# A cross-attention block on one core: the calls of the way in put in another order

## The chip, the cores and the metric

The kernel runs on one core of a Trainium2 chip. The metric is the device time of one execution in microseconds (us). Five engines work side by side, each with its own queue of instructions: TensorE (PE; its weight loads are listed apart as PEld), VectorE (DVE), ScalarE (ACT), GpSimd (POOL) and SyncE (SP), which here does nothing but issue transfers. An engine executes its queue in order; between engines, semaphores make an instruction wait for what it needs.

## The reference, cut to what matters

```python
def _ada_ln(x, c, W_ss, b_ss):
    h = (x - mean(x)) / sqrt(var(x) + EPS)
    scale, bias = split(silu(c) @ W_ss + b_ss, 2)
    return (1.0 + scale)[:, None, :] * h + bias[:, None, :]

xq = _ada_ln(x_q, t_vec, Wss_q, bss_q)
xkv = _ada_ln(x_kv, t_vec, Wss_kv, bss_kv)
q = (xq @ Wq + bq).reshape(B, Lq, nh, dh)
kv = (xkv @ Wkv + bkv).reshape(B, Lkv, 2, nh, dh)
k, v = kv[:, :, 0], kv[:, :, 1]
scores = einsum('bqhd,bkhd->bhqk', q, k) / sqrt(dh)
out = einsum('bhqk,bkhd->bqhd', softmax(scores), v).reshape(B, Lq, H)
return x_q + (out @ Wp + bp)
```

Here B = 16, Lq = 1024, Lkv = 64, H = 512, nh = 16 and dh = 32, all in fp32. `t_vec` is one conditioning vector for each batch.

## The kernel before

**Tiling.** The queries are cut into 32 blocks (`NB`) of 512 rows, two for each batch. A block is held as four tiles of 128 rows, t = 0 to 3. The context is taken in two groups, "A" (batches 0 to 7) and "B" (8 to 15), of 8 × 64 = 512 rows each. They go through the same helpers as a block: load (`load_x`), statistics (`q_stats`), scale (`first_scale`, `q_scale`), normalisation (`hidden`), transposition (`turned_features` on PE for A and B, `turned_products` for block 0, `turn` on DVE with the transfers of `move` for the other blocks), and the scale and shift from the conditioning vector (`modulated`, `turned_scaled`, `scale_features`).

**Products.** Each projection, of q, k, v and of the output, is a 512 × 512 × 512 product done with seven products of half size instead of eight (`seven`, L526, matmul at L544; `product`, L932, matmul at L950), 8 matmuls each. The seven are taken in an order written out by hand, and their operands are partly sums and differences of halves: `column_sums` forms those of the weights on POOL, `feature_sums` those of the features (on DVE for A, on POOL for the others), `weight_sums` and `row_sums` those of the output projection on POOL. Their results are copied out or added up by `context_out`, `query_out`, `query_added` and `added`.

**Attention.** `score_products(i, z)` (matmul at L663) makes the scores of one half z of the keys of block i, with 32 × 32 tiles. `maximum` (DVE) and `copied` (ACT) read them; `maxima`, `subtract` (POOL), `weights` (ACT, the exponential), `total` (POOL), `row_total` and `inverse_rows` (DVE and four small transfers), `mix` (PE, L831) and `divided` (DVE) make the rest. In the notes below "score half" is one `score_products`.

**Tiles that are shared.** Four of them matter here.

- PSUM pool `ps_s` has two slots, each a pair of banks `[P, 2, TB]`. In `turned_features` the transposed tiles t = 0 and t = 2 are the two halves of one such tile, t = 1 and t = 3 of the other; `modulated(i, k, n, eng)` reads t = 2n when `eng` is VectorE and t = 2n + 1 when it is ScalarE. Semaphores follow the whole tile: a write to one half waits for the reads of the other half that stand ahead of it in the order, and a read of one half waits for a write of the other that stands ahead of it.
- The `x` slots are two, so `load_x(1)` waits until `turned_products` has read `x_0`, and `load_x(2)` until `turned_features("B", ·)` has read `x_B`.
- The slot `WT` holds `stage_A`, then `stage_B` (V on its way to `value_move`, 16 transfers for each group), then the weight sums `WT` of the output projection.
- `sum_0` (written by `total(0)`, read by `row_total(0)`) and the copied scores `s_1_0` share the slot `big2`.

```python
if t < 2:
    spares[i, t] = ps_s.tile([P, 2, TB], F32, tag="s", name=f"pxk_{i}_{t}")
turned[i, t] = spares[i, t % 2][:, t // 2, :]
...
t = 2 * n if eng is nc.vector else 2 * n + 1
...
src = turned[i, t][:, at : at + LKV]
```

**The order.** No planner runs in the kernel: each engine's queue holds its instructions in the order in which the Python calls stand. The calls of L987 to L1407, the way in, bring the groups A and B and the blocks 0 to 2 to the point where the loop over `i in range(3, NB - 2)` (L1409) can start. The loop interleaves the scores of block i with the output projection of block i − 2, the mix of i − 1 and the queries of i + 1. So at the end of the way in, block 0 is in its output projection, block 1 in its mix, block 2 in its softmax and block 3 has its queries.

Of the kernel before, what the change touches and what calls it, by code (L numbers as in the profile page):

```python
# [20 lines left out]
def cross_attention_block(  # L21
# [18 lines left out]
    nc = tc.nc  # L40
# [946 lines left out]
    column_sums("k", w_k_sb, w_k_sums, (2,))  # L987
    q_stats("A", (0,))
    q_stats("A", (1,))
    scale_shift_rows("kv", 0)  # L990
    first_scale(0)
    hidden("A", (0,))
    biases()
    scale_shift_taken("kv", 0)
    scale_shift("kv", 2 * NC, 0)
    turned_features("A", 0)
    hidden("A", (1,))
    column_sums("k", w_k_sb, w_k_sums, (0,))
    turned_features("A", 1)
    column_sums("k", w_k_sb, w_k_sums, (1,))  # L1000
    modulated("A", 0, 0, nc.scalar)
    modulated("A", 0, 0, nc.vector)
    q_stats("A", (3,))
    load_x("B")
    q_stats("A", (2,))
    first_scale(1)
    hidden("A", (2,))
    hidden("A", (3,))
    context_product("A", "k", 1)
    scale_shift_rows("kv", 1)  # L1010
    scale_shift_taken("kv", 1)
    turned_features("A", 2)
    context_out("A", "k", 1)
    column_sums("v", w_v_sb, wv_sums, (0,))
    scale_shift("kv", 2 * NC, 1)
    column_sums("v", w_v_sb, wv_sums, (2,))
    modulated("A", 1, 0, nc.vector)
    turned_features("A", 3)
    modulated("A", 1, 1, nc.vector)
    modulated("A", 1, 0, nc.scalar)  # L1020
    modulated("A", 0, 1, nc.scalar)
    modulated("A", 1, 1, nc.scalar)
    context_product("A", "k", 2)
    context_product("A", "v", 1)
    modulated("A", 0, 1, nc.vector)
    context_product("A", "v", 2)
    context_out("A", "k", 2)
    context_out("A", "v", 1)
    feature_sums("A", nc.vector, (0,))
    feature_sums("A", nc.vector, (1,))  # L1030
    feature_sums("A", nc.vector, (2,))
    column_sums("v", w_v_sb, wv_sums, (1,))
    load_query_weights()
    q_stats(0, (0,))
    context_out("A", "v", 2)
    context_product("A", "k", 7)
    context_out("A", "k", 7)
    scale_shift_rows("q", 0)
    context_product("A", "v", 6)
    q_stats(0, (2,))  # L1040
    q_stats(0, (3,))
    q_stats(0, (1,))
    q_scale(0)
    context_product("A", "v", 7)
    feature_sums("A", nc.vector, (3,))
    scale_shift_rows("q", 1)
    context_product("A", "k", 6)
    load_x(1)
    scale_shift_taken("q", 0, 2)
    hidden(0, (2,))  # L1050
    hidden(0, (3,))
    column_sums("v", w_v_sb, wv_sums, (3,))
    context_out("A", "v", 6)
    q_stats("B", (0,))
    q_stats("B", (2,))
    hidden(0, (1,))
    scale_shift("q", 0, 0, 2)
    context_product("A", "v", 5)
    hidden(0, (0,))
    column_sums("k", w_k_sb, w_k_sums, (3,))  # L1060
    q_stats("B", (1,))
    context_out("A", "v", 7)
    q_stats("B", (3,))
    column_sums("q", w_q_sb, w_q_sums, (0,))
    context_out("A", "v", 5)
    turned_products()
    context_out("A", "k", 6)
    context_product("A", "k", 5)
    context_product("A", "v", 3)
    turned_scaled(2)  # L1070
    context_out("A", "k", 5)
    q_scale("B")
    turned_scaled(3)
    column_sums("q", w_q_sb, w_q_sums, (2,))
    turned_scaled(1)
    turned_scaled(0)
    hidden("B", (0,))
    load_x(2)
    q_stats(1, (0,))
    hidden("B", (3,))  # L1080
    hidden("B", (1,))
    feature_sums(0, nc.gpsimd, (0,))
    q_stats(1, (2,))
# [5 lines left out]
    value_move("A", 0)  # L1089
    column_sums("q", w_q_sb, w_q_sums, (1,))  # L1090
    q_stats(1, (1,))
    context_out("A", "k", 3)
    hidden("B", (2,))
# [5 lines left out]
    feature_sums(0, nc.gpsimd, (1,))  # L1099
    modulated("B", 0, 0, nc.scalar)  # L1100
    context_product("A", "k", 4)
    context_out("A", "k", 4)
    modulated("B", 1, 1, nc.scalar)
    query_product(0, 1)
    context_product("B", "k", 1)
    modulated("B", 0, 1, nc.vector)
    context_out("A", "v", 4)
    modulated("B", 1, 1, nc.vector)
    modulated("B", 0, 1, nc.scalar)
    modulated("B", 1, 0, nc.vector)  # L1110
    feature_sums(0, nc.gpsimd, (2,))
    q_scale(1)
    load_projection_bias()
    query_seed(0)
    modulated("B", 1, 0, nc.scalar)
    hidden(1, (0,))
    query_product(0, 6)
    query_product(0, 2)
    context_out("B", "k", 1)
    hidden(1, (1,))  # L1120
    turn(1, (0,))
    column_sums("q", w_q_sb, w_q_sums, (3,))
    feature_sums("B", nc.gpsimd, (0,))
    turn(1, (1,))
    hidden(1, (2,))
    turn(1, (2,))
    hidden(1, (3,))
    feature_sums(0, nc.gpsimd, (3,))
    turn(1, (3,))
    query_out(0, 2)  # L1130
    context_product("B", "k", 2)
    context_out("B", "k", 2)
    q_stats(2, (0,))
    query_product(0, 7)
    q_stats(2, (1,))
    move(1, two=True)
    query_out(0, 6)
    q_stats(2, (2,))
    context_product("B", "k", 7)
    query_out(0, 7)  # L1140
    feature_sums("B", nc.gpsimd, (1,))
    q_stats(2, (3,))
    context_out("B", "k", 7)
    q_scale(2)
    hidden(2, (0,))
    feature_sums("B", nc.gpsimd, (2,))
    query_product(0, 5)
    feature_sums("B", nc.gpsimd, (3,))
    hidden(2, (1,))
    query_product(0, 4)  # L1150
    query_added(0, 5)
    q_stats(3, (0,))
    hidden(2, (2,))
    query_product(0, 3)
    context_product("B", "k", 6)
    query_added(0, 4)
    q_stats(3, (1,))
    q_stats(3, (3,))
    query_out(0, 3)
    score_products(0, 0)  # L1160
    context_out("B", "k", 6)
    hidden(2, (3,))
    copied(0, 0, 1)
    scale_features(1, (1,))
    value_move("A", 1)
    maximum(0, 0, 0)
    turn(2, (0,))
    scale_features(1, (0,))
    scale_features(1, (2,))
    copied(0, 0, 0)  # L1170
    context_product("B", "k", 5)
    turn(2, (1,))
    turn(2, (2,))
    context_product("B", "k", 4)
    turn(2, (3,))
    scale_features(1, (3,))
    maximum(0, 0, 1)
    query_product(1, 1)
    query_seed(1)
    q_stats(3, (2,))  # L1180
    context_out("B", "k", 5)
    feature_sums(1, nc.gpsimd, (0,))
    q_scale(3)
    score_products(0, 1)
    feature_sums(1, nc.gpsimd, (1,))
    load_x(4)
    hidden(3, (0,))
    maximum(0, 1, 1)
    query_product(1, 2)
    context_product("B", "k", 3)  # L1190
    maximum(0, 1, 0)
    query_out(1, 2)
    feature_sums(1, nc.gpsimd, (2,))
    query_product(1, 7)
    context_out("B", "k", 3)
    feature_sums(1, nc.gpsimd, (3,))
    maxima(0)
    hidden(3, (3,))
    q_stats(4, (0,))
    copied(0, 1, 1)  # L1200
    move(2)
    load_projection()
    context_product("B", "v", 1)
    context_out("B", "k", 4)
    copied(0, 1, 0)
    query_out(1, 7)
    subtract(0, zs=(0,))
    context_out("B", "v", 1)
    q_stats(4, (2,))
    hidden(3, (1,))  # L1210
    q_stats(4, (3,))
    query_product(1, 6)
    context_product("B", "v", 2)
    load_x(5)
    q_stats(4, (1,))
    query_out(1, 6)
    weights(0, 0)
    query_product(1, 5)
    hidden(3, (2,))
    scale_features(2, (3,))  # L1220
    scale_features(2, (2,))
    query_product(1, 4)
    subtract(0, zs=(1,))
    context_out("B", "v", 2)
    weights(0, 1)
    context_product("B", "v", 7)
    query_added(1, 5)
    turn(3, (0,))
    query_product(1, 3)
    query_out(1, 3)  # L1230
    turn(3, (1,))
    scale_features(2, (1,))
    total(0)
    scale_features(2, (0,))
    turn(3, (2,))
    turn(3, (3,))
    context_product("B", "v", 6)
    move(3)
    context_out("B", "v", 7)
    query_added(1, 4)  # L1240
    score_products(1, 0)
    context_out("B", "v", 6)
    maximum(1, 0, 1)
    row_total(0)
    maximum(1, 0, 0)
    context_product("B", "v", 5)
    q_scale(4)
    inverse_rows(0)
    load_residual(0)
    query_product(2, 1)  # L1250
    copied(1, 0, 1)
    copied(1, 0, 0)
    query_seed(2)
    feature_sums(2, nc.gpsimd, (0,))
    hidden(4, (0,))
    context_out("B", "v", 5)
    feature_sums(2, nc.gpsimd, (1,))
    feature_sums(2, nc.gpsimd, (2,))
    score_products(1, 1)
    context_product("B", "v", 3)  # L1260
    maximum(1, 1, 0)
    nc.gpsimd.tensor_tensor(b_diff, b_second, b_first, ALU.subtract)
    query_product(2, 2)
    maximum(1, 1, 1)
    copied(1, 1, 1)
    maxima(1)
    copied(1, 1, 0)
    hidden(4, (1,))
    context_out("B", "v", 3)
    mix(0)  # L1270
    feature_sums(2, nc.gpsimd, (3,))
    subtract(1, zs=(1,))
    scale_features(3, (0,))
    query_product(2, 6)
    value_move("B", 0)
    spread_rows(0)
    query_out(2, 2)
    hidden(4, (2,))
    q_stats(5, (0,))
    context_product("B", "v", 4)  # L1280
    biased(0, 2)
    q_stats(5, (3,))
    context_out("B", "v", 4)
    divided(0)
    turn(4, (0,))
    subtract(1, zs=(0,))
    q_stats(5, (1,))
    query_out(2, 6)
    turn(4, (1,))
    query_product(2, 7)  # L1290
    weights(1, 1)
    row_sums(0, 0)
    query_product(2, 5)
    query_out(2, 7)
    turn(4, (2,))
    scale_features(3, (1,))
    scale_features(3, (2,))
    scale_features(3, (3,))
    weights(1, 0)
    product(0, 2)  # L1300
    hidden(4, (3,))
    query_product(2, 4)
    query_added(2, 5)
    query_product(2, 3)
    product(0, 1)
    turn(4, (3,))
    q_stats(5, (2,))
    query_added(2, 4)
    added(0, 1)
# [308 lines left out]
```

## Time and profile before

| | |
|---|---|
| median of 3 runs | 1024.17 us (1024.11 to 1024.31) |
| the profiled execution | 1026.66 us |
| its span | 1024.9 us |
| mean granted clock of TensorE | 0.998 |
| moved by DMA | 149.82 MB, mean 146 GB/s |
| costliest group on POOL: `subtract`, L722 | 64 of 4563 ns |
| costliest group on PE: `product`, L950 | 744 matmuls of 379 ns |

The profile is of one execution. A row of the time line has its start, its duration, the engine and line, what it writes and reads, how many instructions it holds, and in brackets the idle time of the engine ahead of it with what ended that time. A row for a stretch has its span, the busy time of PE, PEld, DVE, ACT and POOL, the granted clock of PE, and the load of the DMA engines. In all of them times are from the start of the span.

### The profile page before, as it was taken

The page shows a single profiled execution, that of the slowest core. Times are in us where ns is not written, and L with a number is a line of the kernel's source. Part 1 is how long each engine was busy: PE and PEld are TensorE (multiplying, and loading weights), DVE is VectorE, ACT ScalarE, POOL GpSimd, SP SyncE. Part 2 cuts the span into 40 slices and gives each one's busy share as a digit, 9 for nine tenths or more (in the row PEclk, how much of TensorE's full clock was granted, in tenths as well). Part 3 has the DMA queues.
Part 4 walks back from the last instruction along what each step waited for, and adds up shares of the span by engine and source line. Part 5 has one row for each costly group of instructions (what it writes and reads, how often), then busy time and mean ns, then how long its engine had stood idle before and what let it go on. Part 6 is the DMA issues. An engine that isn't in the chain of part 4 may idle for free.

```text
span 1024.9 us, 21278 instructions
## 1 busy us (share of the span) xinstructions
PE 1008.3 (98%) x8101; PEld 768.9 (75%) x8101; DVE 863.4 (84%) x1181; ACT 639.2 (62%) x1025; POOL 810.2 (79%) x522
## 2 busy tenths in 40 slices
PE   7899999999999999999999999999999999999998
PEld 6788777787777777777777777777777777777756
DVE  5767789888888888888988898889888988876794
ACT  3677665676666666766667666667676666665530
POOL 3558798889888888889888888898888888987861
PEclk9999999999999999999999999999999999999999
DMA  9466454444555444444553444445544444335122
GB/s 309 155 176 184 113 162 136 156 150 157 158 165 152 133 137 126 155 155 152 166 155 112 153 137 146 155 155 164 164 128 128 123 155 154 117 123 166 45 85 85
DMA packets 112165, 149.82 MB, mean 146 GB/s; under 512 B 34072, under 2 KB 45360, under 8 KB 112064
## 3 DMA queue, kind: packets, MB, share of 16 engines
q1 hardware_dynamic: 111680, 147.94, 46.9%
q8 instruction: 64, 1.05, 0.4%
q0 software_dynamic: 384, 0.54, 0.2%
q14 instruction: 37, 0.30, 0.1%
HBM read 79.21 MB, written 34.60 MB: 111 GB/s over the span
## 4 chain that ended last, share of the span: by engine, by line
PE 92%; DVE 3%; DMA 2%; SPq 2%; POOL 1%; ACT 1%; issue 0%; DVEq 0%; POOLq 0%; ACTq 0%
PE pq L544 38%; PE pp L950 36%; PE ps L663 7%; PE po L831 7%; PE pk_B L544 1%; PE pv_B L544 1%; DMA wss_q<-in_L_xcond_Wss_q_dram 1%; SPq L144 1%; DVE m L680 1%; PE pk_A L544 1%; DMA x<-in_x_dram 1%; PE pv_A L544 1%; SPq L167 1%; POOL s L722 0%; DVE lt L767 0%
## 5 line engine op out<-in xcount | busy, mean ns | idle before, releaser
L722 POOL TENSOR_TENSOR s<-s,mb 128x2048 f32<-128x2048 f32 x64 | 290.4, 4563 | 124.9 <-DVE mb L709 121.6
L689 ACT COPY s<-ps 128x1024 f32<-128x1024 f32 x128 | 129.3, 1012 | 103.8 <-DVE m L680 62.6
L680 DVE TRANSPOSE_TENSOR_REDUCE m<-ps 128x32 f32<-128x1024 f32 x128 | 151.0, 1215 | 32.7 <-PE ps L663 32.6
L950 PE MATMUL pp<-w_p_sb,ot 128*128 128x256 f32 x744 | 171.0, 379 | 0.5 <-DVE r L974 0.4
L974 DVE TENSOR_TENSOR r<-pp,r 128x512 f32<-128x512 f32 x210 | 136.6, 671 | 32.9 <-PE pp L950 28.0
L583 ACT ACTIVATE qt<-pq,bias_t 128x256 f32<-128x256 f32 x256 | 106.0, 465 | 82.9 <-PE pq L544 80.6
L950 PEld LDWEIGHTS pp<-w_p_sb,ot 128*128 128x128 f32 x744 | 141.2, 190 | 20.9 <-issue 1.3
L728 ACT ACTIVATE s<-s 128x2048 f32<-128x2048 f32 x64 | 122.4, 1912 | 40.6 <-POOL s L722 40.3
L762 POOL TENSOR_TENSOR sum<-s,s 128x2048 f32<-128x2048 f32 x31 | 140.7, 4539 | 6.1 <-ACT s L728 6.1
L950 PEld LDWEIGHTS pp<-WT,s 128*128 128x128 f32 x496 | 89.4, 189 | 58.2 <-issue 26.8
L544 PE MATMUL pq<-xt_sums,w_q_sums 128*128 128x256 f32 x512 | 123.8, 385 | 0.0
L950 PE MATMUL pp<-WT,s 128*128 128x256 f32 x496 | 123.2, 391 | 0.2 <-POOL s L929 0.2
L544 PEld LDWEIGHTS pq<-xt_sums,w_q_sums 128*128 128x128 f32 x512 | 94.9, 190 | 36.0 <-issue 24.3
L544 PE MATMUL pq<-xt,w_q_sb 128*128 128x256 f32 x512 | 121.4, 380 | 0.0
L544 PE MATMUL pq<-xt,w_q_sums 128*128 128x256 f32 x512 | 121.1, 379 | 0.0
L950 PE MATMUL pp<-WT,ot 128*128 128x256 f32 x496 | 117.6, 380 | 0.7 <-POOL ot L926 0.6
L544 PEld LDWEIGHTS pq<-xt,w_q_sb 128*128 128x128 f32 x512 | 97.4, 191 | 15.0 <-ACT workq L307 1.7
L544 PEld LDWEIGHTS pq<-xt,w_q_sums 128*128 128x128 f32 x512 | 97.2, 190 | 13.4 <-DVE qt L590 0.2
L950 PEld LDWEIGHTS pp<-WT,ot 128*128 128x128 f32 x496 | 93.8, 190 | 15.3 <-issue 1.6
L341 ACT ACTIVATE x<-x,rstdq 128x512 f32<-128x512 f32 x128 | 97.5, 809 | 3.2 <-POOL rstdq L316 3.2
L452 ACT ACTIVATE xt<-xt,ss_q 128x512 f32<-128x512 f32 x124 | 94.1, 809 | 1.0 <-DMA xt<-ht 0.7
L503 POOL TENSOR_TENSOR xt_sums<-xt 128x512 f32<-128x512 f32 x64 | 81.5, 1273 | 10.2 <-ACT xt L452 7.7
(173 smaller groups left out, 1491.9 us busy)
## 6 DMA issues: line engine op xcount, KB each, us to landing
x<-in_x_dram SPq DMA_DIRECT2D x32, 1024.0 KB, 5.7
r<-in_x_dram SPq DMA_DIRECT2D x32, 1024.0 KB, 5.4
xt<-ht SPq DMA_DIRECT2D x488, 64.0 KB, 2.0
out_dram<-r SPq DMA_DIRECT2D x60, 512.0 KB, 3.7
wss_kv<-in_L_xcond_Wss_kv_dram SPq DMA_DIRECT2D x4, 512.0 KB, 8.9
wss_q<-in_L_xcond_Wss_q_dram SPq DMA_DIRECT2D x4, 512.0 KB, 10.4
vr<-ltd SPq DMA_DIRECT2D x128, 8.0 KB, 1.7
out_dram<-r SPq DMA_DIRECT2D x7, 256.0 KB, 2.1
```

Source lines behind the costliest of these rows:

```text
L341: nc.scalar.activation(dst, src, AF.Identity, bias=rstd[:, 1, j : j + 1], scale=rstd[:, 0, j : j + 1])
L452: nc.scalar.activation(xt[:, :, c, :], xt[:, :, c, :], AF.Identity, scale=ss["q"][:, c, b : b + 1], bias=ss["q"][:, NC + c, b : b + 1],)
L503: eng.tensor_tensor(dst, a, b, ALU.subtract)
L544: nc.tensor.matmul(out_, lhsT=lhsT, rhs=rhs, start=new and m == 0 and c == 0, stop=c == HC - 1, skip_group_check=True,)
L583: nc.scalar.activation(dst, src, AF.Identity, bias=bq_t[:, o : o + 1])
L680: nc.vector.tensor_reduce(m_tiles[i][:, z, 2 * e : 2 * e + 2, :], s_banks[i, z][e].rearrange("p r (j a) -> p r j a", a=32), AX.X, ALU.max, ...
L689: nc.scalar.copy(s_tiles[i, z][:, 2 * e : 2 * e + 2, :], s_banks[i, z][e])
L722: eng.tensor_tensor(s_tiles[i, z], s_tiles[i, z], mb_tiles[i], ALU.subtract)
L728: nc.scalar.activation(p, p, AF.Exp, scale=SCALE)
L762: nc.gpsimd.tensor_tensor(t, s_tiles[i, 0], s_tiles[i, 1], ALU.add)
L950: nc.tensor.matmul(acc[k][:, t * HO : (t + 1) * HO], lhsT=rows[:, c, t * P : (t + 1) * P], rhs=cols[:, c, :], start=n == 2 and t == 0 and ...
L974: nc.vector.tensor_add(r, a, r)
```

## The change

The calls between L987 and L1407 are the same calls with the same arguments, in another order; the file has the same length, and no helper and nothing in the loop or after it is changed. The order of the transfers at the start (the two groups, `x_0`, the weights) on SP stays what it was.

Of the parts that the prediction speaks of, cut to their core:

```diff
-    context_product("A", "k", 2)
     context_product("A", "v", 1)
...
+    context_product("A", "k", 2)
+    context_out("A", "v", 1)
...
+    feature_sums("A", nc.vector, (0,))
     context_product("A", "v", 2)
     context_out("A", "k", 2)
...
+    context_product("A", "v", 7)
+    q_stats(0, (3,))
+    context_product("A", "v", 6)
...
+    turned_products()
     q_stats("B", (0,))
...
+    context_product("A", "v", 5)
...
-    turned_products()
```

The group B, whose `turned_features` come in the order 1, 0, 3, 2 before, with `context_product("A", "v", 4)` ahead of them:

```diff
+    turned_features("B", 0)
...
+    q_stats(1, (0,))
+    turned_features("B", 1)
     q_stats(1, (3,))
-    context_product("A", "v", 4)
-    turned_features("B", 1)
...
+    turned_features("B", 3)
+    q_stats(1, (2,))
...
     q_stats(1, (1,))
...
-    turned_features("B", 0)
+    turned_features("B", 2)
+    modulated("B", 0, 0, nc.scalar)
+    query_product(0, 1)
     modulated("B", 0, 0, nc.vector)
-    turned_features("B", 3)
...
+    context_product("B", "k", 1)
...
-    turned_features("B", 2)
...
+    context_product("A", "v", 4)
```

The scores of block 1 and the sums for the output projection:

```diff
     maximum(1, 0, 1)
     row_total(0)
+    q_scale(4)
+    context_product("B", "v", 5)
+    copied(1, 0, 1)
     maximum(1, 0, 0)
-    context_product("B", "v", 5)
...
+    copied(1, 0, 0)
+    score_products(1, 1)
     inverse_rows(0)
...
+    divided(0)
+    subtract(1, zs=(0,))
...
     context_out("B", "v", 4)
-    divided(0)
...
+    row_sums(0, 0)
     q_stats(5, (1,))
+    total(1)
+    weight_sums(0)
...
+    weight_sums(2)
...
+    value_move("B", 0)
...
+    value_move("B", 1)
...
-    total(1)
...
-    feature_sums(3, nc.gpsimd, (0,))
-    query_product(3, 1)
...
-    weight_sums(0)
-    weight_sums(2)
...
+    product(0, 7)
```

More of the change, by code (lines that the diff above doesn't have):

```diff
@@ L1051, in cross_attention_block @@
-    hidden(0, (3,))
-    column_sums("v", w_v_sb, wv_sums, (3,))
-    context_out("A", "v", 6)
-    q_stats("B", (0,))
[L1055 to L1061, printed above, removed]
+    q_stats(0, (1,))
+    q_stats(0, (2,))
+    context_product("A", "v", 7)
+    q_stats(0, (3,))
+    context_product("A", "v", 6)
+    q_scale(0)
+    hidden(0, (2,))
+    scale_shift_rows("q", 0)
@@ new lines, in cross_attention_block @@
+    copied(2, 1, 1)
+    hidden(5, (3,))
+    product(0, 6)
+    maximum(2, 1, 1)
+    feature_sums(3, nc.gpsimd, (1,))
+    added(0, 6)
+    mix(1)
+    maxima(2)
+    product(0, 5)
+    copied(2, 1, 0)
+    q_stats(6, (0,))
+    scale_features(4, (1,))
+    load_residual(1)
+    hidden(5, (0,))
+    feature_sums(3, nc.gpsimd, (2,))
+    added(0, 5)
+    product(0, 4)
+    query_product(3, 6)
+    query_out(3, 2)
+    hidden(5, (1,))
+    product(0, 3)
+    query_out(3, 6)
+    subtract(2, zs=(0,))
```

513 lines of the change are left out of this document (239 added, 274 removed).

## The prediction

> **What bounds the kernel now.** I read the page's busy line first, then the chain of work that ended last.
>
> ```profile
> PE 1008.3 (98%) x8101; PEld 768.9 (75%) x8101; DVE 863.4 (84%) x1181; ACT 639.2 (62%) x1025; POOL 810.2 (79%) x522
> ...
> PE 92%; DVE 3%; DMA 2%; SPq 2%; POOL 1%; ACT 1%; issue 0%; DVEq 0%; POOLq 0%; ACTq 0%
> ```
>
> TensorE (PE) is the bound. Only its 16.6 us of idle time (1024.9 − 1008.3) and the stretches at a lower clock can be won. The view of stretches shows where they are (span, then busy time of PE, PEld, DVE, ACT, POOL, PE's granted clock, DMA share, GB/s):
>
> ```profile
> 20.00:30.00 10.00, 8.99 (x66) 7.09 (x67) 8.92 (x18) 3.97 (x13) 7.52 (x6) 1.00 1.07 362
> ...
> 46.00:58.00 12.00, 9.71 (x54) 8.52 (x53) 9.03 (x28) 9.39 (x28) 6.67 (x10) 1.00 0.48 124
> ...
> 100.00:120.00 20.00, 18.87 (x155) 13.13 (x154) 16.87 (x18) 11.79 (x18) 16.32 (x13) 0.91 0.55 134
> ...
> 160.00:200.00 40.00, 40.00 (x345) 30.33 (x314) 36.44 (x45) 25.71 (x38) 31.65 (x25) 1.00 0.47 147
> 200.00:300.00 100.00, 100.00 (x831) 76.42 (x831) 88.75 (x118) 66.77 (x104) 85.25 (x50) 1.00 0.47 146
> ```
>
> From 160 us on PE has no gap. The change touches only calls before that, so whatever head start PE has at the first score product of block 3 (I call it sc30, at 159.56) should pass unchanged to the end. In the way in, the table of PE's waits names the losses (us in total, times, longest):
>
> ```profile
> PE pxk_B L407 <- DVE xk_B L424: 2.3, 1, 2.3
> PE pk_A L544 <- ACT xk_A L426: 1.6, 2, 0.8
> PE ps L663 <- ACT s L689: 1.1, 1, 1.1
> ...
> PE pk_A L544 <- DVE xk_sums_A L503: 0.8, 1, 0.8
> ```
>
> **The B stall: the two halves of one tile.** Time line:
>
> ```profile
> 39.95 11.51 SPq L109 DMA_DIRECT2D x<-in_x_dram  x2
> ...
> 45.36 0.69 DVE L298 BATCH_NORM_STATS2 bs<-x 128x6 f32<-128x512 f32 x1 [2.95 <-DMA x<-in_x_dram]
> ...
> 49.17 1.07 DVE L424 TENSOR_SCALAR xk_B<-pxk_B,ss_kv 128x64 f32<-128x64 f32 x4
> 50.38 0.63 PE L407 MATMUL pxk_B<-ident,x_B 128*128 128x128 f32 x4 [2.29 <-DVE xk_B L424]
> ```
>
> `pxk_B` is a pair: t=0 and t=2 are halves of one tile, and semaphores follow the whole tile. Before, `modulated("B", 0, 0, nc.vector)` reads half t=0, and only after it is t=2 written. That read (49.17) stands on DVE behind the four statistics of block 1, which wait until 45.36 for `x_1`. After, `turned_features("B", 2)` stands ahead of every read of this pair, so PE no longer waits: −2.29. The wait is not abolished but turned round: the read of t=0 now waits for the write of t=2, which comes (by my count of products) at 47.6 to 48.1, about 1 us earlier than that read came before. The first product on B starts at 49.85 by the same count, 4.4 us earlier than before, because `context_product("A", "v", 4)` now follows it. `x_1` is issued after `turned_products`, which I put at 37.6 instead of 39.95. Bounds: −2.29 if the reads keep pace; −1.2 if the 1.07 us read has to be waited for. I take −2.29, and +0.2 for a short wait at the second product on B.
>
> **The start of group A.** Before, PE lost 0.8 us three times there (table above). The new order takes `context_product("A", "v", 1)` first, which covers the second wait for `xk_A`, and forms the first feature sum ahead of the K addition, which covers the wait for `xk_sums_A`: −1.6. It adds two: product 6 of V needs `wv_sums` step 1, the last but two of POOL's column sums. These begin when a DMA lands and share time with DVE's sums:
>
> ```profile
> 19.62 2.50 POOL L477 TENSOR_TENSOR w_k_sums<-w_k_sb 128x512 f32<-128x512 f32 x2 [15.88 <-DMA w_k_sb<-in_L_xcond_Wkv_dram]
> ...
> 25.88 1.73 POOL L477 TENSOR_TENSOR wv_sums<-wv_sums,w_v_sb 128x512 f32<-128x512 f32 x1
> 24.75 1.72 DVE L503 TENSOR_TENSOR xk_sums_A<-xk_A 128x512 f32<-128x512 f32 x1
> ...
> 28.18 0.69 DVE L503 TENSOR_TENSOR xk_sums_A<-xk_A 128x512 f32<-128x512 f32 x1
> ```
>
> A sum on DVE takes 1.72 beside a working POOL and 0.69 alone; POOL's takes 1.73 beside it against 2.50 / 2 = 1.25. Six POOL sums from 19.62, 7.5 us, and three collisions of 0.5 to 0.7 put the end at 28.7 to 29.2; product 6 would be ready at 28.4: +0.65. The Trainium skill, "SBUF — State Buffer", section "Who interferes with whom", calls this an exclusive lock (two SBUF inputs on DVE against a GpSimd read); by it each meeting costs up to a whole POOL sum, 1.25, and the trace's 1.72 − 0.69 = 1.03 agrees. At its worst three meetings would then take 3.75 instead of 1.6 to 2.1, product 6 would wait 2.5, and this part would come to +1.4 instead of −0.4. The other new wait is `turned_products`, now ahead of V's product 5: it waits for the last normalised tile of `x_0`, +0.45. What is left, transposes and weight rows shuffled under DMAs that land when they did, I put at +0.1. Sum −0.4; bounds −1.6 (neither new wait) and +1.0 (POOL's sums each collide once more).
>
> So at product 6 of block 0's query PE is 2.7 ahead, and 2.5 at the second score half of block 1, which waits again:
>
> **The stall at block 1's scores.**
>
> ```profile
> 100.88 2.27 DVE L767 TRANSPOSE_TENSOR_REDUCE lt<-sum 128x64 f32<-128x2048 f32 x1
> ...
> 103.23 2.09 ACT L689 COPY s<-ps 128x1024 f32<-128x1024 f32 x2 [3.20 <-PE pq L544]
> ...
> 104.30 0.18 PEld L663 LDWEIGHTS ps<-qt,K_A 32*32 32x32 f32 x16 [1.53 <-ACT s L689]
> 104.30 2.17 PE L663 MATMUL ps<-qt,K_A 32*32 32x512 f32 x32 [1.13 <-ACT s L689]
> ```
>
> The score slots are freed by `copied(1, 0, ·)`, which overwrites the tile that `row_total(0)` (100.88) reads. In the new order DVE still has the total between the two maxima, and POOL's sum before it moves with everything else. So the stall (1.13, and 2.17 instead of 1.14 for the products themselves) moves with PE: 0, bounds −2.2 and 0. Right after it the clock is halved for some 3.4 us:
>
> ```profile
> 107.00:108.00 1.00, 1.00 (x3) 0.73 (x3) 0.97 (x2) 0.09 (x1) 0.41 (x1) 0.50 0.43 103
> ...
> 51.01 1.73 PE pk_A L544 x8
> ...
> 106.47 3.45 PE pv_B L544 x8
> 109.92 1.89 PE pq L544 x8
> ```
>
> A product of 8 matmuls takes 1.73; here one takes 3.45 and the next 1.89: 1.88 lost. The 2.29 us stall at 48 was followed by no such row (clock 1.00 in 46 to 58). The Trainium skill, "TensorE: Matmul & The Clock Gate", "Part 1: The HAM clock gate", has a free-running window of about 3.4 us, and halves the clock after an idle one; the trace's 3.4 us agree. By its rule, whether the stall, moved by 2.5 us, falls into one window is chance. What the loss is worth is the next step.
>
> **POOL's chain to `WT`, the gate that counts.** In the way out of block 0, product 7 reads `WT[:, 2]`:
>
> ```profile
> 116.47 7.12 SPq L636 DMA_DIRECT2D V_B<-stage_B  x9
> ...
> DMA to landing us min/median/max: 2.0/2.6/6.3
> ...
> 124.32 4.53 POOL L762 TENSOR_TENSOR sum<-s,s 128x2048 f32<-128x2048 f32 x1 [1.98 <-ACT s L728]
> 128.82 1.26 POOL L503 TENSOR_TENSOR xt_sums<-xt 128x512 f32<-128x512 f32 x1
> 130.04 1.27 POOL L889 TENSOR_TENSOR WT<-w_p_sb 128x512 f32<-128x512 f32 x1
> 131.28 1.27 POOL L893 TENSOR_TENSOR WT<-w_p_sb 128x512 f32<-128x512 f32 x1
> ...
> 132.65 1.94 PE L950 MATMUL pp<-WT,ot 128*128 128x256 f32 x8
> ...
> 152.11 3.62 PE L950 MATMUL pp<-w_p_sb,ot 128*128 128x256 f32 x16
> ...
> 159.56 1.14 PE L663 MATMUL ps<-qt,K_A 32*32 32x512 f32 x32
> ```
>
> `WT[:, 2]` is done at 132.55 and product 7 starts at 132.65, so before, a full clock would have brought nothing here: the halving is hidden behind POOL. After, the subtractions start 2.5 us earlier with PE, the 1.98 us gap before the total closes because `row_sums(0, 0)` fills it, and the sums of block 2's features (128.82) no longer stand between. I put the total at 119.65 to 124.2. Then `weight_sums(0)` meets a new bound: `WT` lies in the slot of `stage_B`, so it waits for the last of 16 `V_B` transfers. Eight of these still follow the addition of V's product 4, which now stands behind `divided(0)` on DVE; I count their issue from 117.4, and at 7.12 / 9 = 0.79 each they are out at about 123.6. The last may land after 2.0 us, 125.6, and two sums of 1.27 give 128.1. PE is there at 126.9 with a full clock and at 128.8 with a halved one, so product 7 starts at 128.1 or 128.8, against 132.65.
>
> From there I count PE's work. Product 7 of block 0 to product 1 of block 1 took 152.11 − 132.65 = 19.46 and has the same number of pieces after (one query product of block 3 goes in, one comes later): ready at 147.55. It needs the first half of `divided(1)`, which follows `move(4)` on SP and four short DVE pieces: 147.4 to 147.9, I take 147.8. From it to sc30 took 7.45, now with one query product more, 1.73: sc30 at 157.0. That is 2.56 ahead of 159.56.
>
> **The sum** in the profiled execution (1026.66 us, of which the span is 1024.9): −2.29 (B stall) − 0.4 (A) + 0.2 (B's second product) ± 0 (scores) gives −2.5 at the scores; from there the chain through `WT` and `divided(1)` keeps it at −2.56. So 1026.66 − 2.5 = 1024.16. The unprofiled median is 2.49 lower, and I carry the difference over: 1024.17 − 2.5 = 1021.7. DVE (89 of 100 us busy in the loop) and POOL (85) start the loop as far ahead as PE, so neither becomes the bound.
>
> **Rivals.**
>
> 1. *More than that.* The score stall goes too, or the last `V_B` landing isn't waited for: product 7 at 126.9 gives sc30 at 155.8 plus what `divided(1)` then costs, up to 0.9: 3.0 to 3.8 ahead, 1020.8. For it: DVE's work around the total is reordered. Against it: the order total, second maximum stands. Chance 0.12.
> 2. *The change doesn't do what it says.* The wait only changes direction. If the reads of B's first half, now behind the write of t=2, hold the first two products on B by 1 us, and group A gains nothing, PE is 2.29 − 1.07 − 0.2 = 1.0 ahead, and a halved clock that meets no cover later takes the rest: 1023.2 to 1024.2, take 1023.6. For it: whole-tile waits stay in force. Against: two other products cover the read. Chance 0.25.
> 3. *Halved clock in another place.* If the low clock falls where PE is the gate, 1.9 − (128.1 − 126.9) = 0.7 is lost: 1022.4. Chance 0.1.
> 4. *Slower: `V_B` lands late.* Product 7 hangs on the last of 16 small transfers, with a load of 1 MB of `x_6` issued behind. At the longest landing shown, 6.3, `WT[:, 2]` comes at 123.6 + 6.3 + 2.5 = 132.4, product 7 as late as before, and as one more query product then stands behind it (1.73) and `divided(1)` costs nothing, sc30 is at 132.4 + 19.46 + 9.18 = 161.0: 1.5 slower, 1025.7. If the addition before the last issue also comes 1 us later, 1026.7. It decides from a landing after 128.5 (161.0 less 1.5 us): earlier, the kernel is not slower. For it: the slot is shared and nothing else covers this wait. Against: the median landing is 2.6. Chance 0.15.
>
> **How the numbers follow.** Forecast 0.38, rivals 0.12, 0.25, 0.1, 0.15. The predicted time is the forecast's, 1021.7; its own range is 1020.9 to 1022.5. A measurement here can tell about 0.2%, 2.05 us, so faster means below 1022.1. Faster: three quarters of the forecast, all of rival 1, a third of rival 3 and a little of rival 2, 0.48. Slower (above 1026.2): half of rival 4, and small new waits of several engines that none of the steps above names, 0.15. Same: the rest, 0.37. The range goes from rival 1, 1020.3, to rival 4, 1025.7.
>
> **What would show it.** Right: the row `pxk_B <- xk_B` gone or below 0.3 in PE's waits; the score wait still there near 102; product 7 (`pp<-WT,ot`) near 128 with a wait for POOL, the first `WT` sum behind a DMA; sc30 near 157; PE without a gap in every later stretch. Wrong: a new wait of PE over 1 us between 20 and 60, a first `WT` sum after 127, sc30 after 158, or a head start at sc30 that shrinks inside the loop.

## The result, and the profile after

| | before | after |
|---|---|---|
| median of 8 runs | 1024.24 us (1023.87 to 1026.16) | 1021.59 us (1020.64 to 1022.5) |
| ratio after / before | | 0.9967, 95% interval 0.9956 to 0.9977 |
| span of the first profile | 1024.9 us | 1019.7 us |
| span of the second profile | 1025.5 us | 1022.0 us |

The medians differ by 2.65 us; the ratio stands for 3.4 us, and its interval allows 2.4 to 4.5. The forecast was 2.5 us, 1021.7. The profiles differ by more (5.2 and 3.5 us), and a part of this section is about why.

The busy line and the chain of the page of after:

```profile
PE 1006.6 (99%) x8101; PEld 767.5 (75%) x8101; DVE 862.8 (85%) x1181; ACT 638.3 (63%) x1025; POOL 811.4 (80%) x522
...
PE 74%; POOL 3%; DVE 3%; SPq 2%; DMA 2%; ACT 2%; issue 1%; DVEq 0%; POOLq 0%; ACTq 0%
```

PE is busy in 99% of the span, and only 13.1 us are idle (1019.7 − 1006.6) instead of 16.6. That the chain now runs through PE for 74% and not 92% says nothing on the time: it leaves PE wherever another engine was as late as PE. The stretches and the waits of PE:

```profile
20.00:30.00 10.00, 9.84 (x57) 7.70 (x60) 9.85 (x22) 1.84 (x7) 9.84 (x7) 1.00 1.07 363
...
46.00:58.00 12.00, 12.00 (x59) 10.61 (x58) 10.75 (x30) 10.44 (x28) 9.35 (x16) 1.00 0.64 197
...
100.00:120.00 20.00, 20.00 (x169) 14.85 (x154) 18.11 (x26) 14.98 (x22) 15.54 (x7) 1.00 0.44 116
...
160.00:200.00 40.00, 40.00 (x357) 30.16 (x342) 35.84 (x43) 25.51 (x40) 30.64 (x22) 1.00 0.43 130
```

```profile
PE ps L663 <- ACT s L689: 1.1, 1, 1.1
PE pp L950 <- DVE ot L811: 0.9, 1, 0.9
PE pk_A L544 <- ACT xk_A L426: 0.8, 1, 0.8
...
PE pxk_A L407 <- ACT x_A L341: 0.5, 1, 0.5
PE pxt L435 <- DVE ss_q L288: 0.4, 1, 0.4
```

The wait of 2.3 us for the halves of B is gone. The three waits of 0.8 in group A are one; the wait at the second scores of block 1 stands where it stood; a wait for `divided(1)` is new, and one at `turned_products`. (The table lists no wait under 0.15 us; two shorter ones are told of below.) The clock is 1.00 in all of these stretches. Group B on the time line:

```profile
42.78 1.47 PE L407 MATMUL pxk_B<-ident,x_B 128*128 128x128 f32 x12
44.09 1.89 PE L544 MATMUL pk_A<-xk_sums_A,w_k_sb 128*128 128x256 f32 x8
45.82 0.60 PE L407 MATMUL pxk_B<-ident,x_B 128*128 128x128 f32 x4
46.25 1.89 PE L544 MATMUL pq<-xt,w_q_sb 128*128 128x256 f32 x8
...
46.46 2.11 DVE L424 TENSOR_SCALAR xk_B<-pxk_B,ss_kv 128x64 f32<-128x64 f32 x8 [1.31 <-PE pxk_B L407]
```

The transposition of t = 2 starts at 45.82 without a gap. It is now DVE that waits for it, 1.31 us, and nobody waits for DVE: the wait is turned round, as the prediction had it, and costs nothing.

To compare executions I cut the way in at eight starts: the first column sum of POOL (it begins when `w_k` has landed, so most of the luck of the first transfers lies ahead of it), products 7 and 6 of K of group A ("K7", "K6"), product 6 of block 0's query ("q06"), the second scores of block 1, the mix of block 0, sc30, and the end. The first column is a start, every other one the difference of two starts, all from the time line of PE and POOL; the last is the sum from the first column sum to sc30.

| kernel | column sum | to K7 | to K6 | to q06 | to scores | to mix | to sc30 | to end | sum to sc30 |
|---|---|---|---|---|---|---|---|---|---|
| before | 19.62 | 7.00 | 7.57 | 21.84 | 48.27 | 7.43 | 47.83 | 865.34 | 139.94 |
| before, 2nd | 19.13 | 6.99 | 7.57 | 23.36 | 48.26 | 5.75 | 49.22 | 865.22 | 141.15 |
| before, 3rd | 18.01 | 6.98 | 8.04 | 21.67 | 48.27 | 7.44 | 47.48 | 867.31 | 139.88 |
| after | 18.68 | 5.14 | 7.61 | 20.01 | 48.26 | 5.75 | 49.04 | 865.21 | 135.81 |
| after, 2nd | 20.36 | 5.13 | 7.60 | 20.01 | 48.27 | 5.75 | 49.22 | 865.66 | 135.98 |

Three things can be read from it. The first transfers land at 18.0 to 20.4 whatever the kernel, so a single pair of profiles can be wrong by 2 us. Behind that, after gains 1.86 us up to K7 and 1.7 to 3.4 between K6 and q06, and next to nothing later. And before loses another 1.5 to 1.7 us to the halved clock in each of its three profiles, but at two different places (21.84 against 23.36, or 5.75 against 7.43).

### The profile page after: what moved, and what is told of

It reads as the page before. It is cut to its first block, busy times and chain, and to the rows that moved or that the text cites. A ratio compares the mean times of both kernels' runs of the same rounds, so it can differ in the third digit from the quotient of the medians.

```text
span 1019.7 us, 21267 instructions
## 1 busy us (share of the span) xinstructions
PE 1006.6 (99%) x8101; PEld 767.5 (75%) x8101; DVE 862.8 (85%) x1181; ACT 638.3 (63%) x1025; POOL 811.4 (80%) x522
## 4 chain that ended last, share of the span: by engine, by line
PE 74%; POOL 3%; DVE 3%; SPq 2%; DMA 2%; ACT 2%; issue 1%; DVEq 0%; POOLq 0%; ACTq 0%
PE pp L950 32%; PE pq L544 31%; PE ps L663 6%; PE po L831 5%; SPq L394 2%; POOL s L722 1%; DMA x<-in_x_dram 1%; ACT s L728 1%; POOL xt_sums L503 1%; DVE m L680 1%; DVE mb L709 0%; DVE l L733 0%; DMA xt<-ht 0%; ACT xt L452 0%; ACT qt L583 0%
## 5 line engine op out<-in xcount | busy, mean ns | idle before, releaser
L950 PE MATMUL pp<-w_p_sb,ot 128*128 128x256 f32 x744 | 171.3, 379 | 1.4 <-DVE ot L811 0.9
L950 PEld LDWEIGHTS pp<-w_p_sb,ot 128*128 128x128 f32 x744 | 141.1, 190 | 22.1 <-ACT qt L583 1.3
L950 PEld LDWEIGHTS pp<-WT,s 128*128 128x128 f32 x496 | 89.4, 189 | 58.2 <-issue 28.5
L950 PE MATMUL pp<-WT,s 128*128 128x256 f32 x496 | 123.2, 391 | 0.2 <-POOL s L929 0.2
L950 PE MATMUL pp<-WT,ot 128*128 128x256 f32 x496 | 117.5, 380 | 0.7 <-POOL ot L926 0.6
L950 PEld LDWEIGHTS pp<-WT,ot 128*128 128x128 f32 x496 | 93.9, 190 | 15.1 <-POOL ot L926 1.0
```

Source lines behind the costliest of these rows:

```text
L950: nc.tensor.matmul(acc[k][:, t * HO : (t + 1) * HO], lhsT=rows[:, c, t * P : (t + 1) * P], rhs=cols[:, c, :], start=n == 2 and t == 0 and ...
```

## The experiments

Each edit is in the order of calls only, unless said otherwise.

**Both kernels again.** The same files, for more profiles.

> The kernel before once more, for a second profile of it. In the first profiles before and after differ by 5.2 us of span (1024.9 against 1019.7), in the medians by 2.65. Theory 'unlucky start': the first profile of before had a late first transfer (its x_B was issued at 22.47, that of after at 21.52) and lost some 1 us by it, and the rest at the halved clock behind the second scores of block 1; then the second profile has a span near 1022.5, x_B near 21.5 and no row at clock 0.50. Rival 'the profile costs before more': span 1024.5 or more again, with the row at clock 0.50.

> The changed kernel once more, for a second profile. Expected by both theories: no wait of PE for xk_B, the wait of 1.1 us at the second scores of block 1, the first product of block 0 with WT near 125, about 0.9 us of wait for divided(1), sc30 (first scores of block 3) at 154 to 156 depending on the first transfers. If the clock is halved behind the scores in this one, the halving is chance and not part of the change.

> The kernel before a third time. Its clock was halved once behind the scores of block 1 and once behind the stall of B; in six profiles of kernels without a stall of over 1.2 us in group B never. Theory 'a stall of 2 us trips it, at a place that the phase decides': again one row of 3 to 4 us at clock 0.50 behind one of the two. Rival 'chance of its own': no row below 0.9, or one at a place without a stall.

The theory of an unlucky start fell: the second profile of before has a span of 1025.5, the third one of 1025.2, and their column sums start earlier than in the first. What held is the halving. The second profile of after has a late start itself (20.36), and by it a wait of over 1 us, which the prediction had named as a sign of being wrong:

```profile
25.49 1.97 PE L544 MATMUL pk_A<-xk_sums_A,w_k_sums 128*128 128x256 f32 x8 [1.61 <-DVE K_A L610]
```

DVE waits there 1.06 us for the bias of V (`b_v_sb`), and K7 for DVE. As POOL's column sums are as late, K7 comes 5.13 us behind the first of them, as in the first profile, so this is the start and not the order.

Back to the halving. Stretches of the second profile of before, behind the stall of B:

```profile
51.00:52.00 1.00, 1.00 (x3) 0.79 (x3) 0.00 (x0) 0.94 (x6) 0.00 (x0) 0.50 0.46 80
52.00:53.00 1.00, 1.00 (x4) 0.76 (x3) 0.00 (x0) 0.34 (x3) 0.51 (x3) 0.50 0.77 244
```

and of the third, behind the scores again:

```profile
106.00:107.00 1.00, 1.00 (x4) 0.81 (x3) 0.93 (x3) 0.42 (x1) 0.07 (x1) 0.50 0.42 98
107.00:108.00 1.00, 1.00 (x4) 0.81 (x3) 1.00 (x1) 1.00 (x2) 0.00 (x0) 0.50 0.00 0
```

In the second profile, where the clock is whole behind the scores, the time line has at block 0's way out:

```profile
119.23 2.35 DVE L811 TENSOR_TENSOR ot<-po,vb 128x1024 f32<-128x1024 f32 x2
...
121.68 1.97 PE L950 MATMUL pp<-w_p_sb,ot 128*128 128x256 f32 x8 [1.17 <-issue]
```

Product 1 of block 0 waits 1.17 us, and no releaser is named; `ot` is its only late operand, and `divided(0)` ends writing it at 121.58. So a halving behind the scores, 1.68 us in the column "to mix", is given back in the next column, all but 0.3 in the first profile and wholly in the third; one behind the stall of B, 1.5 us in the column "to q06", isn't.

**The halves alone.** One call moved in each kernel.

```diff
 before
     turned_features("B", 0)
+    turned_features("B", 2)
     modulated("B", 0, 0, nc.vector)
     turned_features("B", 3)
     load_x(3)
-    turned_features("B", 2)
 after
+    modulated("B", 0, 0, nc.vector)
     turned_features("B", 2)
     modulated("B", 0, 0, nc.scalar)
     query_product(0, 1)
-    modulated("B", 0, 0, nc.vector)
```

> Before, with one call moved: turned_features('B', 2) ahead of modulated('B', 0, 0, nc.vector), so that the write of the second half stands ahead of the reads of the first. Theory 'the halves alone': PE's wait of 2.3 us for xk_B is gone and everything behind it comes 2.3 us earlier, 1024.2 - 2.3 = 1021.9, about the whole measured gain. Rival 'taken up later': the wait goes, but the reads of B on DVE, still behind the statistics of block 1, become the next wait of PE (first product of B), and the end gains 0.5 us or less: 1023.7 or more.

> After, with one call moved: modulated('B', 0, 0, nc.vector) ahead of turned_features('B', 2), so that the write waits for the reads of the other half again. Theory 'the halves alone': the wait of about 2.3 us comes back, 1021.6 + 2.3 = 1023.9. Theory 'x_1 earlier': in the new order DVE is through with the statistics of block 1 at 45.1, so the reads end at 46.2 and PE, there at 45.8, waits 0.4 us: 1021.6 to 1022.0.

In before, the one move gave 0.9979 (0.9968 to 0.9989), 1022.64 us against 1025.26 in the same comparison. In after, taking it back gave 0.9973 (0.9962 to 0.9984), not to be told from after's 0.9967. The rows of PE, of before with the move and of after without it:

```profile
44.94 1.91 PE L407 MATMUL pxk_B<-ident,x_B 128*128 128x128 f32 x16
46.69 1.89 PE L544 MATMUL pk_A<-xk_sums_A,w_k_sb 128*128 128x256 f32 x8
```

```profile
45.79 0.63 PE L407 MATMUL pxk_B<-ident,x_B 128*128 128x128 f32 x4 [0.30 <-DVE xk_B L424]
```

So the order of the halves is worth the whole stall in the old order, and in the new one a wait of 0.30 us (0.49 in the column "to q06", 20.50 against 20.01). There `x_1` is loaded earlier, DVE is through with its statistics when the halves are read, and a product of K stands on PE between the transposition of t = 3 and that of t = 2. This kernel doesn't part the two; the next one, without that product, comes nearer to the load alone.

**Group A alone.** First all of the new order up to group B, then the three calls that I held to be its gain.

```diff
 before, three calls moved
+    context_product("A", "v", 1)
     context_product("A", "k", 2)
-    context_product("A", "v", 1)
...
+    context_out("A", "v", 1)
+    feature_sums("A", nc.vector, (0,))
     context_out("A", "k", 2)
-    context_out("A", "v", 1)
-    feature_sums("A", nc.vector, (0,))
```

> Group A in the new order: the calls of after up to turned_features('B', 0), and from there all the others in the order of before (so t=2 of B is again written behind the reads of t=0). In the profiles so far, from POOL's first column sum (when w_k has landed) to product 6 of K of group A it is 14.56 to 14.66 us in the order of before and 12.73 to 12.75 in that of after. Theory 'two gains': group A's 1.85 come (12.75) and the stall of B comes back wholly or in part, since the rest is in the order of before, so 1 to 2.5 us faster than before. Rival 'A is luck of the first transfers': 14.6, and no gain above 0.5.

> Before, with three calls of group A moved: product 1 of V ahead of product 2 of K, and the output of product 1 of V and the first feature sum ahead of the K addition. Theory 'the two covered waits': PE loses its waits at product 2 of K (0.8) and product 7 of K (0.8), so from POOL's first column sum to product 6 of K it takes 12.7 to 13.0 us instead of 14.6; the stall of B shrinks by some of it or not, since x_1 comes earlier too. Rival 'POOL's order of the weight sums is the gain': 14.0 or more, since POOL's order stays that of before.

The first gave 0.9959 (0.9946 to 0.9971), the second 1.0001 (0.9992 to 1.0011). The rows of PE of the second say where its gain went:

```profile
23.61 1.97 PE L544 MATMUL pk_A<-xk_sums_A,w_k_sums 128*128 128x256 f32 x8
25.50 0.41 PE L260 MATMUL ss_q<-wss_q,early 128*32 128x128 f32 x4
26.66 1.07 PE L260 MATMUL ss_q<-wss_q,early 128*32 128x128 f32 x28 [0.74 <-DMA wss_q<-in_L_xcond_Wss_q_dram]
...
48.53 0.63 PE L407 MATMUL pxk_B<-ident,x_B 128*128 128x128 f32 x4 [2.31 <-DVE xk_B L424]
48.99 3.31 PE L544 MATMUL pk_A<-xk_sums_A,w_k_sb 128*128 128x256 f32 x8
```

K7 starts 5.22 us after the first column sum instead of 7.00, so the three calls are the gain there. Then the weight rows of q, which in this order come next, aren't all landed (0.74 us; the new order puts products 7 and 6 of V ahead of them), so that K6 comes after 13.92 us and not the 12.7 to 13.0 expected, the stall of B is as long as ever, and the clock is halved behind it (3.31 for a product of 1.73). In the first of the two kernels, with all of the new group A, `turned_products` and so `x_1` come earlier and the stall of B is down to 0.85, for a read on ACT. So the earlier load takes 1.4 us of the 2.3, not all:

```profile
46.78 0.63 PE L407 MATMUL pxk_B<-ident,x_B 128*128 128x128 f32 x4 [0.85 <-ACT xk_B L426]
```

**Both small edits, and a mixture.** The three calls of A and the one of B together in before; and the new group A with the one move of B, the rest as before.

> Before, with both small edits: the three moved calls of group A and the one of group B (t=2 written ahead of the reads of t=0). Theory 'the whole gain is these two': as fast as after, 1.8 us at product 6 of K and 2.1 between it and product 6 of the query, 3.4 to 4.5 us faster than before in one comparison of medians. Rival 'the rest of the 420 calls carries a part of over 1 us': 1 us or more slower than after, that is 2.5 us faster than before or less.

> Group A in the order of after, the rest in that of before, with t=2 of B written ahead of the reads of t=0. In the run without that move PE still waited 0.85 us for the reads. Theory 'order of the halves': the wait goes, product 6 of K to product 6 of the query takes 20.2 us instead of 21.05, and product 6 of K to sc30 122.2 instead of 123.0, 0.9 less than in after (123.1). Rival 'taken up later': 122.8 to 123.1.

| kernel | column sum | to K7 | to K6 | to q06 | to scores | to mix | to sc30 | to end | sum to sc30 |
|---|---|---|---|---|---|---|---|---|---|
| t=2 first | 17.85 | 6.97 | 7.69 | 19.71 | 48.37 | 5.75 | 48.68 | 865.88 | 137.17 |
| three calls of A | 18.39 | 5.22 | 8.70 | 23.55 | 48.27 | 5.75 | 47.77 | 866.45 | 139.26 |
| both | 18.55 | 5.14 | 8.45 | 19.69 | 48.37 | 5.75 | 48.15 | 867.10 | 135.55 |
| new A, rest before | 18.64 | 5.14 | 7.61 | 21.05 | 48.26 | 5.75 | 47.95 | 865.40 | 135.76 |
| new A, t=2 first | 18.93 | 5.14 | 7.60 | 20.35 | 48.38 | 5.75 | 47.54 | 865.11 | 134.76 |
| after, read first | 18.19 | 5.14 | 7.61 | 20.50 | 48.27 | 5.75 | 48.79 | 865.81 | 136.06 |

Four moved calls bring the way in to 135.55 us, as short as the 135.81 and 135.98 of after with its 420. The mixture is 1.0 to 1.2 shorter still. The times don't contradict this, but they can't show it: 0.9974 (0.9963 to 0.9984) for the four calls, 2.7 us and below the 3.4 to 4.5 that I expected, though inside after's interval, so that a part of about 1 us for the other calls isn't ruled out; and 0.9972 (0.9959 to 0.9986) for the mixture, so its further us can be seen in the profile alone.

**The stalls that were left.** In after: V's last addition ahead of `divided(0)`; the scores of block 1 without their stall; both.

```diff
 edit 1
     context_out("B", "v", 3)
+    context_out("B", "v", 4)
...
-    context_out("B", "v", 4)
 edit 2
     maximum(1, 0, 1)
-    row_total(0)
...
     maximum(1, 0, 0)
+    row_total(0)
...
-        pool, tag = (xpool, "x") if i == NB - 2 else (big, f"big{(i + 1) % 2 * 2}")
+        pool, tag = (xpool, "x") if i == NB - 2 else (big, f"big{(i + 1) % 2 * 2}" if i else "big3")
```

> After, with one call moved: context_out('B', 'v', 4) directly behind context_out('B', 'v', 3), ahead of divided(0), so that the last eight V_B transfers are issued some 4 us earlier, and move(4) and the transfers of 1/l for divided(1) behind them on SP some 2 us earlier. Theory 'SP is the bound of product 1 of block 1': its wait of 0.9 to 1.1 us for divided(1) goes, and product 7 of block 0 to the first scores of block 3 takes 28.7 us instead of 29.5 to 29.7. Rival 'DVE's own order holds divided(1)': wait and stage stay.

> After, without the stall at the second scores of block 1: sum_0 lies in the slot big3 instead of big2, and row_total(0) stands behind maximum(1, 0, 0). Both theories: PE's wait of 1.1 us for the copied scores goes and the products take 1.1 instead of 2.2, so the mix of block 0 comes 2.0 to 2.2 us earlier. Theory 'PE's order is all': sc30 too, 2 us faster than after. Theory 'SP holds divided(1)': divided(1) stays where it was in time, its wait grows from 0.9 to about 2.5 to 3, and sc30 gains 0 to 0.3.

> Both edits together. Theory 'SP holds divided(1)': now the gain of the scores passes on, and sc30 is 2.0 to 2.6 us earlier than in after, against 0.9 by the first edit alone and 0 to 0.3 by the second. Theory 'PE's order is all': 2 + 0 = the gain of the second edit alone. A wait at product 1 of block 0 for divided(0), up to 0.4 us, may show.

| kernel | column sum | to K7 | to K6 | to q06 | to scores | to mix | to sc30 | to end | sum to sc30 |
|---|---|---|---|---|---|---|---|---|---|
| edit 1 | 18.41 | 6.37 | 7.23 | 20.04 | 48.27 | 5.75 | 48.60 | 865.03 | 136.26 |
| edit 2 | 18.24 | 5.31 | 7.43 | 20.01 | 47.07 | 4.75 | 50.72 | 865.77 | 135.29 |
| both | 18.05 | 6.36 | 7.24 | 20.03 | 47.07 | 4.75 | 50.29 | 865.61 | 135.74 |

Edit 2 takes 2.2 us out of the two columns around the scores, and 1.5 to 1.7 of them come back before sc30. The rows of PE, and of DVE, of that kernel:

```profile
98.06 1.18 PE L663 MATMUL ps<-qt,K_A 32*32 32x512 f32 x32
...
124.00 1.99 PE L950 MATMUL pp<-WT,ot 128*128 128x256 f32 x8 [0.69 <-POOL WT L893]
```

```profile
96.97 2.27 DVE L767 TRANSPOSE_TENSOR_REDUCE lt<-sum 128x64 f32<-128x2048 f32 x1
99.16 0.65 DVE L629 TENSOR_TENSOR stage_B<-pv_B,stage_B 128x512 f32<-128x512 f32 x1
99.73 0.53 DVE L782 RECIPROCAL lt<-lt 128x64 f32<-128x64 f32 x1
100.19 2.31 DVE L680 TRANSPOSE_TENSOR_REDUCE m<-ps 128x32 f32<-128x1024 f32 x2
```

DVE runs without a gap from the first maxima (94.66) to the spread ones (102.86); to move the total behind a maximum doesn't shorten that queue. So POOL's subtractions, its total and the sums of `WT` come hardly earlier, and PE, now 2 us ahead, waits for them. Edit 1 halves the wait for `divided(1)` (0.47 instead of 0.90), where I had expected it to go: SP is earlier by 2 us, but DVE starts `vb`, which `divided(1)` reads, only 0.4 earlier, counted from the scores (139.95 − 100.32 against 139.73 − 99.70): its queue ahead of that has gaps of 0.2 us at most from 133.52 on, and two additions and two transpositions stand between `vb` and `divided(1)`. So the rival theory of that run, DVE's own order, is the other half. Both together gain 0.9 to 1.1 from q06 to sc30 (102.11 against 103.05 and 103.24), half of what I had expected. The ratios of the three, 0.995, 0.9943 and 0.9946 (intervals of about 0.0012 on each side), are lower than after's, but against another set of runs of before (median 1026.83); their medians of 1021.0 to 1021.5 lie within 0.6 of after's. I don't call them faster. The jump of the column "to K7" in edit 1 and in both, 6.36 against 5.14, isn't theirs either, since nothing ahead of K7 was changed: DVE's first feature sum starts 0.8 to 1.0 us later behind POOL's first column sum there, meets one more of POOL's column sums and has to let it pass.

## Why the prediction was right

**The B stall.** Right in kind and size: −2.29 forecast; the one move in before shortens "to q06" by 2.13 (21.84 to 19.71; 1.96 against the third profile of before). What the prediction gave no weight to is that `x_1`, 2.4 us earlier by its own count, takes 1.4 us of the stall without any move of the halves.

**The start of group A.** The two covered waits were right: 1.86 to K7, −1.6 forecast. Of the two new ones, that for `turned_products` came (0.42 against 0.45); that of product 6 of V came too, but as 0.37 instead of 0.65, and from K7 to K6 the new order loses next to nothing (7.60 against 7.57), as its weight rows of q now run in one piece. This is the term that was mis-sized: −0.4 forecast, −1.8 + 0.4 = −1.4 measured. K7 in before, then K7 and the rows of DVE, POOL and PE around it in after:

```profile
26.62 1.97 PE L544 MATMUL pk_A<-xk_sums_A,w_k_sums 128*128 128x256 f32 x8 [0.79 <-DVE xk_sums_A L503]
```

```profile
23.82 1.97 PE L544 MATMUL pk_A<-xk_sums_A,w_k_sums 128*128 128x256 f32 x8
...
22.06 1.01 DVE L503 TENSOR_TENSOR xk_sums_A<-xk_A 128x512 f32<-128x512 f32 x1
23.00 0.68 DVE L610 TENSOR_TENSOR K_A<-pk_A,K_A 128x512 f32<-128x512 f32 x1
23.60 1.15 DVE L503 TENSOR_TENSOR xk_A<-xk_A 128x512 f32<-128x512 f32 x1
...
22.48 3.40 POOL L477 TENSOR_TENSOR wv_sums<-w_v_sb 128x512 f32<-128x512 f32 x2
25.96 1.60 POOL L477 TENSOR_TENSOR wv_sums<-wv_sums,w_v_sb 128x512 f32<-128x512 f32 x1
...
25.62 3.99 PE L544 MATMUL pv_A<-wv_sums,xk_sums_A 128*128 128x256 f32 x16
```

K7 starts 0.14 us behind the end of the K addition (23.68): it waits for that now, and hardly. The sums of DVE take 1.0 to 1.2 here and not 1.72, because each meets what is left of a sum of POOL and not the whole of one. POOL is done with step 1 at 27.56, 8.9 us after its start. Products 7 and 6 of V, one row here, take 3.99 instead of 3.62: product 6 starts at 27.62, just behind step 1, and the 0.37 us are its wait, of which the view counts too little to list it. The Trainium skill, "SBUF — State Buffer", "Who interferes with whom", calls such a meeting an exclusive lock; these rows agree: the first two sums of DVE end 0.54 us behind the sum of POOL that they met (at 23.07 and 24.75, POOL's at 22.53 and 24.21), and the phase decides how much of 1.25 us is paid.

So the −1.4 isn't fixed either. Of the eight profiles with all of the new group A, six have K6 12.7 us behind the first column sum and two, edit 1 and both, 13.6, where DVE had to let one more sum of POOL pass; before has 14.6 and once 15.0.

**B's second product.** The +0.2 was not there: q06 to the scores takes 48.26 to 48.27 in both kernels.

**The scores of block 1.** Right: the wait is 1.13 in both, and it moved with PE. The halved clock behind them cost 1.68 us in before (7.43 against 5.75), not 1.88: a row of 1.89 is what every whole product has, since a row's end overlaps the next row.

**The clock.** The prediction left open whether a halving comes (product 7 at 128.1 or 128.8). None came in ten profiles of kernels without the long stall of B, but the clocks listed with the other runs show that this was luck in part (see the last section). What covers a halving behind the scores was named wrongly. The prediction had POOL's chain to `WT` hide it. In the second profile of before, with a whole clock there, product 7 did not wait for `WT`; what had waited was product 1, for `divided(0)`.

**POOL's chain to `WT`.** The path was right and its price too high. Rows of SP, POOL and PE of after:

```profile
107.34 13.28 SPq L636 DMA_DIRECT2D V_B<-stage_B  x16
...
117.71 4.55 POOL L762 TENSOR_TENSOR sum<-s,s 128x2048 f32<-128x2048 f32 x1
122.30 1.27 POOL L889 TENSOR_TENSOR WT<-w_p_sb 128x512 f32<-128x512 f32 x1
123.54 1.26 POOL L893 TENSOR_TENSOR WT<-w_p_sb 128x512 f32<-128x512 f32 x1
...
124.86 1.99 PE L950 MATMUL pp<-WT,ot 128*128 128x256 f32 x8
...
145.68 1.97 PE L950 MATMUL pp<-w_p_sb,ot 128*128 128x256 f32 x8 [0.90 <-DVE ot L811]
...
154.49 1.14 PE L663 MATMUL ps<-qt,K_A 32*32 32x512 f32 x32
```

Product 7 starts 0.05 us behind the second sum of `WT`, in both profiles of after, so POOL's chain is its gate. But it lost 0.2 and 0.3 us by it, not 1.2: the product ahead of it took 2.05 and 2.17 until product 7 started, where 1.83 is usual. It started at 124.86, not 128.1; of these 3.2 us, 0.9 are the earlier first transfers, 1.2 the gain up to the scores beyond the 2.5 forecast, and 1.1 are this step's own error. The last `V_B` was issued by 120.62 instead of 123.6 and landed at 122.09, just ahead of the total's end at 122.26. The first sum of `WT` starts 0.21 behind that landing in both profiles, 0.1 to 0.2 later than it stands behind the total where `V_B` lands early (after, read first). So the landing may have cost 0.2 us, and hardly more. Then `divided(1)` cost 0.9 and 1.1 where I took 0.25, as SP's `move(4)` stands ahead of its transfers. From the scores to sc30 it took 54.79 and 54.97, against 55.26, 54.97 and 54.92 in before: nothing in sum, as forecast (−0.06), by other terms than forecast.

**From sc30 to the end.** 865.2 and 865.7, against 865.2 to 867.3: what PE has gained at sc30 reaches the end, as far as the loop's own spread lets one see it. That PE has no gap from 160 us on isn't true of the end (it waits 0.7 us at L858 and 0.6 at L950), but the gaps are alike in both.

**The sum.** By the columns −1.4 (A), −2.1 (B) and 0 to −1.5 for the halved clock, 3.5 to 5; by the last column of the table 3.9 to 5.3, where the forecast had 2.56 at sc30 (it came at 154.49, or 155.4 if the first transfers had been as late as in before, and not at 157.0). The medians say 2.65, the ratio 2.4 to 4.5. So the forecast of 2.5 lies at the low end, since A was taken too small by 1.0, and that it meets the medians within 0.2 is luck in part. Why the medians show less than the profiles stays open; the first transfers differ from run to run, and two of the eight runs of after list a clock of 0.998, as the profiles with a halving do. Of the rivals, that of a late `V_B` came to 0.2 us at most, and the stall of the scores, whose end the first rival counted as gain, turned out to be worth 0.5 to 0.7 of its 2.2 us.

## What to carry to other kernels

When two halves of a tile share their semaphores, look at what stands ahead of the read on the reading engine: the write of the other half waits for that, here for the statistics of another block's load. One call moved cures it; the load earlier takes a part of it. And when a stall on the bounding engine is removed, ask which queue next to it had no gap: 2.2 us at the scores were worth 0.5 to 0.7, as DVE had no gap there.

## What the runs showed of the hardware

The clock. Each of the four profiles with a stall of 2.1 to 2.3 us in group B has one stretch of 3.41 us at clock 0.50, two of them right behind that stall and two behind the scores of block 1; none of the ten others has one between the start and the last products, though eight of these have the same wait of 1.1 us at the scores. Where the stall falls decides it, as far as these profiles go. All changes of the clock in the 14 traces lie at whole multiples of 3.413 us behind the first record of a full clock, the four halvings at 12, 13, 29 and 29 times that. In the window of this grid ahead of a halving, PE is idle for 2.11 us (second profile of before) or 2.31 (three calls of A), or the wait at the scores and all 32 of its small matmuls (32 × 32) lie in it, with 0.30 or 0.18 us of other PE work (first and third profile of before). No halving follows where a window has 1.87 or 1.71 us of the stall of B and the next or last one the rest (third and first of before), nor where the window with the scores holds 0.76 us of other work (after, read first) or more (all others). That small matmuls count for little is argued from these windows alone. The Trainium skill, "TensorE: Matmul & The Clock Gate", "Part 1: The HAM clock gate", asks for an idle window of about 3.4 us; here 2.1 us of idle time, or 1.0 to 1.1 us beside the scores, were enough, so the trace doesn't agree on that point, while the length of the low stretch does.

So a halving isn't bound to the stall of B. The mean clocks listed with the runs say the same: one halving takes 1.7 of some 1022 us, the four profiles with one list 0.997 or 0.998, the ten others 0.999 or 1.0. At 0.998 or less are 43 of 63 runs of before, and 33 of 77 of the kernels without the long stall, among them 8 of 12 of "t=2 first" and 2 of the first 8 of after. Where in these runs the clock was low isn't known.

The first transfers. POOL's first column sum, which waits for `w_k`, started between 17.85 and 20.36 in 14 profiles whose first transfers are issued in the same order. The medians of before, 1024.24, 1025.26, 1025.98 and 1026.83 in four comparisons, differ by as much as the change is worth, so only ratios within one comparison can be compared.

The loop. From sc30 to the end it took 865.0 to 865.9 in eleven profiles and 866.5, 867.1 and 867.3 in three; in those three PE waits 0.9 to 1.8 us for `qt` from ACT, in no more than three places. The cause is open.
